# The last tile's expert sums, last C weighting and gating on VectorE, and two experts of the tile before it, in a new instruction order

## The chip, the core and the metric

The kernel runs on one core of a Trainium2 chip. The core's engines take their instructions in order, each from its own queue: TensorE (PE; its weight loads are a row of their own, PEld), VectorE (DVE), ScalarE (ACT), GpSimd (POOL), and SyncE (SP), whose queue issues the DMAs. They meet through semaphores only. The metric is the device time of one execution in microseconds; a kernel's time is the median of its runs.

## What is computed

One layer over x of 32 sequences x 256 tokens x 128 channels, float32: a Mamba block and a mixture of experts, each behind a LayerNorm and with a residual.

```python
# x: (32, 256, 128); 256 inner channels, 16 states, 8 experts of 256 hidden units
xr = layernorm(x) @ W_in;  xi, res = split(xr)
u = silu(causal_conv4(xi) + conv_b)
dbc = u @ W_x                       # delta (rank 8), B (16), C (16)
delta = softplus(dbc[:, :8] @ W_dt + b_dt)
h_t = exp(delta * A) * h_(t-1) + delta * B * u     # for each channel and state
y = sum_n(h * C) + u * D
x = x + (y * silu(res)) @ W_out

s = layernorm(x) @ gate_w.T;  cw = softmax over the top 2 of 8 scores, 0 elsewhere
x = x + sum_e cw[:, e] * (silu(layernorm(x) @ w1[e].T) @ w2[e].T)
```

## The kernel before, in words

**Tiles.** The sequences are cut into 17 tiles: tile 0 and tile 16 hold one sequence (256 tokens), tiles 1 to 15 two (512). A tile's work is cut into pieces with short names, `i:name` for tile i. The text `ORDER` (L47 to L283) is one list of all pieces, written out; L1144 to L1147 run through it, and each piece appends its instructions to its engines' queues. So the order of the list is each engine's order of work, and the relation between engines is set by what waits for what. The order runs three to four tiles side by side: the scans of tile i, the experts of tile i-1, the first half of tiles i+1 and i+2.

**First half.** `ldx` loads x (L373; two buffers, shared with `ldr`, which loads it again for the residual), `st1*`, `sa1`, `rs1`, `ap1` are the LayerNorm (L538 to L563), `tr1`, `hi1`, `nl1`, `lo1` transpose it and split it into a high and a low part, since the large products run as three products of split float32 (`PARTS`). `cv` is the convolution folded into W_in (L635; `km`, `kh`, `kl` prepare its weights, `kw` those of the experts' first layer, `kwr` and `kdt` two others), `u` its SiLU, `gp`, `gs` the gate silu(res), `wx`, `sb`, `rh`, `nr`, `rl`, `zz`, `sp` lead to delta, and `bcd` writes B and C to DRAM, from where `rb` and `rc` load rows of them spread over all partitions (L778; four buffers each).

**Scans.** A tile has 16 scans (tile 0 and 16: 8), each over 1024 elements of 128 partitions. For scan k: `dk` (ScalarE, L760) makes exp(delta*A) into one of nine buffers; `in` (VectorE, L812) multiplies delta*u, held in PSUM, by B; `sc` (VectorE, L819) scans; `cm` (GpSimd, L830) multiplies by C; `ys` (TensorE, L834) adds up in PSUM, transposing. h has three buffers, so a scan waits for the ysum three scans earlier. After each half of the scans `yc` (ScalarE) copies y, `yz` (GpSimd, L911) multiplies it by the gate, `yt` (TensorE) and `ye` (ScalarE) transpose it, `px` and `op` (TensorE, L934 and L941) add the residual and the product with W_out in PSUM, and `x2` (ScalarE, L954) copies the sum.

**Experts.** `st2*`, `sa2`, `rs2`, `ap2`, `tr2`, `hi2`, `nl2`, `lo2` are the second LayerNorm; `gt` (TensorE) the scores; `sc`, `r0` to `r4`, `rx`, `rw0` to `rw4` rank and weigh them on VectorE, GpSimd and, for the exp, ScalarE: rw1 and rw2 (VectorE) wait for rw4 (GpSimd), rw3 (GpSimd) for rw2. For expert e: `wi` (TensorE, L1079, two halves), `si` (ScalarE, L1092), `wo` (TensorE, L1100) into a PSUM tile pe, `as` (ScalarE, L1112) scales pe by the weight into so, one instruction for 128 tokens, and `aa` (GpSimd, L1118) adds so to x2. `sto` stores x2 (L1141). All these PSUM tiles share four buffers of the pool `ps_w`; a new tile takes one that the pieces before it in the list have released.

**Function tables.** ScalarE's exp, SiLU and softplus are in different tables. `need` (L527 to L531) loads one (L530) where the order changes from one to another.

Of the kernel before, what the change touches and what calls it, by code (L numbers as in the profile page):

```python
# [8 lines left out]
F32 = mybir.dt.float32  # L9
# [5 lines left out]
P = 128  # L15
# [32 lines left out]
0:pm 0:ldx 0:lw0 0:lc0 0:lc1 0:ldk 0:lw1 1:ldx 0:ldg 0:st10 0:st11 0:l11 0:sa1 0:ldd 0:rs1 0:ldp 0:km0 0:ap1  # L48
3:ldx 0:tr1 0:l10 0:km1 0:hi1 0:nl1 0:kh1 0:lo1 0:kl1 0:kh0 0:cv1 0:kl0 1:st10 1:st12 1:st13 0:ka 1:st11 1:sa1
1:rs1 0:cv0 0:u1 1:ap1 0:kdt 2:ldx 1:tr1 0:u0 0:kwr 0:wx 0:gp0 0:sb 3:st10 0:rh 0:bcd 1:hi1 0:nr 0:ldo 0:rl  # L50
1:nl1 0:gs0 0:zz 1:lo1 0:pb0 0:kw0 0:sp0 1:cv0 0:pc0 0:rb1 0:rc0 0:rc1 2:st10 0:rb2 0:dq0 0:rb3 2:st13 0:in0
0:rc2 0:rc7 0:ld2 0:dk0 0:kw1 1:cv1 0:dk1 0:sc0 0:dk5 2:st12 0:cm0 0:in1 0:dk2 2:st11 2:sa1 0:sc1 0:dk4 0:kdg
0:rc3 2:rs1 0:ys0 0:dk3 0:in2 0:cm1 0:dk6 0:sc2 0:in3 0:cm2 1:u1 1:u0 3:st11 0:sc3 2:ap1 1:wx 0:ys1 0:dq1 1:rh
0:in6 1:sb 1:bcd 0:ys2 0:sc6 1:nr 1:gp0 1:gs0 1:rl 0:in4 1:zz 0:cm3 1:gp1 1:rb1 3:st13 0:sc4 1:rb5 1:sp0 0:ldr
1:sp1 0:pt 0:ys3 1:du0 0:in5 0:yc0 0:cm4 1:rb4 0:sc5 0:dk7 0:yz0 0:ys4 0:in7 0:kgt 1:dk3 0:cm6 0:yt0 1:dk0
# [232 lines left out]
def mamba_moe_kernel(  # L288
# [938 lines left out]
```

## Time and profile before

| | us |
|---|---|
| median of 3 runs | 1052.45 (1048.1 to 1054.97) |
| the profiled execution | 1053.02 |
| its span, first to last instruction | 1051.3 |
| mean granted TensorE clock | 0.982 of full speed |
| busy: TensorE, weight loads | 964.2, 843.7 |
| busy: VectorE, ScalarE, GpSimd | 956.8, 946.6, 914.0 |
| first scan starts, last scan ends | 28.16, 1012.26 |

A row of a timeline has the start in us, the duration, the engine, the line, the operation, the tile written and those read, their shapes, how many instructions the row holds and, in brackets, how long the engine stood idle before it and what released it. A row with a window has for each engine the busy microseconds and the instructions in it. Durations of pipelined instructions overlap: sixteen output-layer matmuls of 0.28 us take 1.79 us together.

### The profile page before, as it was taken

Reading aid. Unit: us, or ns where it says so; the run is one execution under the profiler, and the core shown is the slowest. Engines: PE = TensorE matmul, PEld = TensorE weight load, DVE = VectorE, ACT = ScalarE, POOL = GpSimd, SP = SyncE. Lnnn points to the kernel's source line nnn. Section 1 sums busy time; section 2 is a strip of 40 time slices with the busy share of each in tenths; the row PEclk is TensorE's granted clock in tenths of the full one; section 3 lists DMA queues with packets and bytes.
Section 4 is the critical chain, followed back from the end, with each engine's and each line's share of the span. In section 5 each row is a group of like instructions: output and inputs, shape, how many; then the busy total and the mean of one; then the engine's idle time right before and its main releaser. Section 6 shows DMA issues by size and latency. Waiting matters only on the chain.

```text
span 1051.3 us, 18971 instructions
## 1 busy us (share of the span) xinstructions
PE 964.2 (92%) x6757; PEld 843.7 (80%) x6757; DVE 956.8 (91%) x903; ACT 946.6 (90%) x1914; POOL 914.0 (87%) x688
## 2 busy tenths in 40 slices
PE   6578789999999999999999999999899999999998
PEld 4467667979888887978888887978778888887898
DVE  3999999999999999999999999999999999999950
ACT  6867989999899998999999898989989998899977
POOL 2577788979989999989999999998989999899975
PEclk9879999999999999999999999999999999999999
DMA  5565848658486775758577684848667584776500
GB/s 180 192 225 173 282 149 281 238 183 275 159 249 220 243 268 192 265 165 283 194 263 247 197 284 140 285 176 282 231 215 252 191 286 159 256 233 201 172 11 17
DMA packets 86095, 223.75 MB, mean 213 GB/s; under 512 B 8049, under 2 KB 35313, under 8 KB 85873
## 3 DMA queue, kind: packets, MB, share of 16 engines
q1 hardware_dynamic: 86000, 222.55, 63.7%
q8 instruction: 53, 0.87, 0.3%
q14 instruction: 42, 0.34, 0.1%
HBM read 217.28 MB, written 5.24 MB: 212 GB/s over the span
## 4 chain that ended last, share of the span: by engine, by line
PE 34%; ACT 29%; DVE 18%; POOL 10%; issue 7%; DMA 1%; SPq 0%; DVEq 0%; POOLq 0%; ACTq 0%
DVE h L819 11%; ACT da L760 11%; PE pf L1079 10%; PE y L834 7%; POOL h L830 6%; PE pe L1100 6%; DVE db L812 6%; ACT L530 5%; ACT so L1112 4%; ACT hs L1092 3%; PE pc L635 3%; POOL x L1118 2%; PE po L941 1%; PE pg L703 1%; PE pd L658 1%
## 5 line engine op out<-in xcount | busy, mean ns | idle before, releaser
L830 POOL TENSOR_TENSOR h<-h,rc 128x1024 f32<-128x1024 f32 x256 | 607.1, 2381 | 62.1 <-DVE h L819 52.2
L819 DVE TENSOR_TENSOR_SCAN h<-da,db 128x1024 f32<-128x1024 f32 x256 | 584.5, 2283 | 25.5 <-PE y L834 7.8
L760 ACT ACTIVATE da<-de,a_sb 128x510 f32<-128x510 f32 (+1 forms) x544 | 341.1, 714 | 0.9 <-DVE h L819 0.4
L812 DVE TENSOR_TENSOR db<-du,rb 128x1024 f32<-128x1024 f32 x256 | 314.9, 1230 | 10.5 <-ACT du L799 2.3
L834 PE MATMUL y<-ident,h 128*128 128x128 f32 x2048 | 268.6, 277 | 16.4 <-POOL h L830 16.0
L834 PEld LDWEIGHTS y<-ident,h 128*128 128x128 f32 x2048 | 237.0, 143 | 37.9 <-POOL h L830 25.7
L1100 PE MATMUL pe<-w_sb,hs 128*128 128x128 f32 x2048 | 249.3, 277 | 9.4 <-ACT so L1112 3.0
L1100 PEld LDWEIGHTS pe<-w_sb,hs 128*128 128x128 f32 x2048 | 237.8, 192 | 16.7 <-ACT so L1112 4.9
L1079 PE MATMUL pf<-xt,w_r 128*128 128x512 f32 (+1 forms) x816 | 215.8, 398 | 14.1 <-DVE rank L1028 6.4
L1079 PEld LDWEIGHTS pf<-xt,w_r 128*128 128x128 f32 x816 | 138.3, 189 | 53.8 <-ACT hs L1092 15.5
L1092 ACT ACTIVATE hs<-pf 128x512 f32<-128x512 f32 (+1 forms) x272 | 143.8, 577 | 40.6 <-PE pf L1079 37.4
L1118 POOL TENSOR_TENSOR x<-x,so 128x512 f32<-128x512 f32 (+1 forms) x136 | 166.0, 1221 | 13.3 <-ACT so L1112 12.3
L1112 ACT ACTIVATE so<-pe,cw 128x128 f32<-128x128 f32 x512 | 147.4, 390 | 4.2 <-PE pe L1100 2.0
L530 ACT ACT_TABLE_LOAD x101 | 129.6, 1283 | 1.8
L635 PE MATMUL pc<-xt_r,wc_r 128*128 128x512 f32 (+1 forms) x408 | 101.0, 399 | 2.7 <-ACT xt_r L624 0.9
L635 PEld LDWEIGHTS pc<-xt_r,wc_r 128*128 128x128 f32 x408 | 74.6, 198 | 18.6 <-issue 2.0
L911 POOL TENSOR_TENSOR g<-yt,g 128x512 f32<-128x512 f32 (+1 forms) x34 | 41.4, 1218 | 7.5 <-ACT yt L904 7.5
L793 POOL TENSOR_TENSOR dus<-de,u 128x512 f32<-128x512 f32 (+1 forms) x32 | 40.3, 1260 | 6.6 <-ACT de L739 6.6
L851 PE MATMUL y<-dg_sb,u 128*128 128x128 f32 x256 | 35.7, 282 | 8.3 <-ACT yt L904 4.2
L851 PEld LDWEIGHTS y<-dg_sb,u 128*128 128x128 f32 x256 | 32.7, 194 | 12.9 <-ACT yt L904 7.5
L941 PEld LDWEIGHTS po<-wo_sb,yt 128*128 128x128 f32 x256 | 31.2, 195 | 4.2 <-issue 2.9
L941 PE MATMUL po<-wo_sb,yt 128*128 128x128 f32 x256 | 32.7, 280 | 0.8 <-ACT yt L922 0.8
(95 smaller groups left out, 705.6 us busy)
## 6 DMA issues: line engine op xcount, KB each, us to landing
rc<-bc SPq DMA_DIRECT2D x205, 512.0 KB, 5.1
rb<-bc SPq DMA_DIRECT2D x187, 512.0 KB, 4.7
xa<-in_x SPq DMA_DIRECT2D x15, 256.0 KB, 4.5
xc<-in_x SPq DMA_DIRECT2D x15, 256.0 KB, 5.5
out<-x SPq DMA_DIRECT2D x15, 256.0 KB, 5.0
w1h<-in_w_t SPq DMA_DIRECT2D x2, 512.0 KB, 5.0
bc<-s SPq DMA_DIRECT2D x32, 32.0 KB, 2.2
w_sb<-in_w_t SPq DMA_DIRECT2D x1, 1024.0 KB, 10.8
```

The lines of the kernel that those rows point to most:

```text
L530: nc.scalar.preload_act_table_set(SETS[which])
L635: nc.tensor.matmul(pcv, wc_r[a][:, j, c * P : (c + 1) * P], xt1_r[b][:, : nb[i], o + j : o + j + L], start=(k == 0), stop=(k == 3 * KC - 1),)
L760: nc.scalar.activation(da[:, m, :, 1:], de[:, :, 1:], AF.Exp, scale=a_sb[:, c, n : n + 1])
L812: nc.vector.tensor_mul(db, d["du"].unsqueeze(1).to_broadcast([P, gs[i], tok[i]]), rows["b", i, k])
L819: nc.vector.tensor_tensor_scan(flat(h), da_of(i, k), flat(d["db"]), 0.0, ALU.mult, ALU.add,)
L830: nc.gpsimd.tensor_tensor(h, h, rows["c", i, k], ALU.mult)
L834: nc.tensor.matmul(y[:, q, :], src[:, q * P : (q + 1) * P], ident, is_transpose=True, start=False, stop=last, skip_group_check=True,)
L1079: nc.tensor.matmul(pf, w1_r[a][:, e, f * P : (f + 1) * P], d["xt"][b], start=(k == 0), stop=(k == 2),)
L1092: nc.scalar.activation(d["hs", e][:, f, :], d["pf", e, f], AF.Silu)
L1100: nc.tensor.matmul(pe[:, q, :], hs[:, f, q * P : (q + 1) * P], w2_sb[:, e, f, :], start=(f == 0), stop=(f == FC - 1),)
L1112: nc.scalar.activation(so[:, q, :], d["pe", e][:, q, :], AF.Copy, scale=d["cw"][:, q, e : e + 1])
L1118: nc.gpsimd.tensor_tensor(x2, x2, st[i]["so", e], ALU.add)
```

## The change

A second form of some pieces is added, and the list is another one throughout. What the last tiles do differently:

- The last scan of tile 16 is weighted by C on VectorE (`cn7`, a new piece) and not on GpSimd (`cm7`).
- The second half's gating in tile 16 is one product on VectorE (`yv1`, new), which reads y from PSUM, in place of ScalarE's copy (`yc1`) and GpSimd's product (`yz1`).
- The eight experts of tile 16, and experts 6 and 7 of tile 15, are weighted and added to x2 by VectorE (`ad`, one scalar_tensor_tensor for each 128 tokens, reading pe from PSUM), in place of `as` on ScalarE and `aa` on GpSimd: 16 + 8 instructions.
- `ad` pieces are now there for all experts. Pieces `st3*`, `xd`, `lv2` and `yv0` and the branch in `op` for a tile without `px` are added too; the list doesn't use them.

All other pieces are in the list as before, at other places. The list is cut here to lines that the text speaks of.

```diff
--- before
+++ after
 ORDER = """
-0:pm 0:ldx 0:lw0 0:lc0 0:lc1 0:ldk 0:lw1 1:ldx 0:ldg 0:st10 0:st11 0:l11 0:sa1 0:ldd 0:rs1 0:ldp 0:km0 0:ap1
-3:ldx 0:tr1 0:l10 0:km1 0:hi1 0:nl1 0:kh1 0:lo1 0:kl1 0:kh0 0:cv1 0:kl0 1:st10 1:st12 1:st13 0:ka 1:st11 1:sa1
-1:rs1 0:cv0 0:u1 1:ap1 0:kdt 2:ldx 1:tr1 0:u0 0:kwr 0:wx 0:gp0 0:sb 3:st10 0:rh 0:bcd 1:hi1 0:nr 0:ldo 0:rl
...
-3:in11 2:rw4 3:cm10 3:ys9 2:rw1 4:sp0 3:rb14 3:sc11 4:sp1 2:wi50 2:wi70 4:du0 3:rc15 3:ys10 2:si70 3:in12
...
-12:as7 13:ys13 13:in15 15:hi1 13:cm14 14:dk0 15:nl1 12:wo2 16:st11 14:rb1 13:sc15 14:rc1 14:dp0 13:ldr 15:lo1
...
-12:wo3 14:rc7 13:st23 14:sc4 12:as0 14:dk12 14:ys2 12:aa4 14:rc5 13:st21 14:dk13 14:ys3 14:in5 14:ldr 14:cm4
...
-15:si50 15:wi51 16:cm4 16:yc0 15:wi31 15:si60 16:sc5 15:wi20 15:si31 15:si51 15:wi70 15:r4 15:si20 16:yz0
-16:ys4 14:aa2 16:in7 15:wi00 15:rx 15:rw4 16:sc7 15:wi11 16:cm5 15:wo5 15:si70 15:si00 15:rw1 15:rw2 16:yt0
-15:rw3 16:px 16:cm7 15:as5 16:ys5 15:si11 16:ys6 16:ye0 15:wi01 14:aa4 16:ys7 15:wo1 14:sto 16:yc1 15:si01
-16:yz1 15:aa5 16:yt1 15:wi21 16:ye1 16:op 15:wo0 16:st20 16:x2 16:st21 15:si21 16:sa2 15:as1 16:rs2 15:wi71
...
-16:si60 16:si40 16:wi50 16:rx 15:as6 15:wo7 16:rw4 15:aa4 16:rw1 16:rw2 16:rw3 15:aa6 16:wi41 16:wo0 16:si50
-15:as7 16:wo2 16:as0 16:wi70 16:si41 16:wi51 16:aa0 16:si70 16:wi71 16:si51 15:aa7 16:wo4 16:si71 16:as2
-16:wi11 16:wo7 15:sto 16:as4 16:si11 16:aa4 16:wi61 16:wo1 16:as7 16:aa2 16:wo5 16:as1 16:aa7 16:si61 16:wo3
-16:aa1 16:as5 16:wo6 16:aa5 16:as3 16:aa3 16:as6 16:aa6 16:sto
...
+0:pt 0:pm 0:ldx 0:lw0 0:lc0 0:lc1 1:ldx 0:ldk 0:ldd 0:ld2 0:lw1 0:st10 0:st11 0:sa1 0:rs1 0:ap1 3:ldx 0:ldo
+0:ldp 0:l11 0:l10 0:km1 0:tr1 0:km0 0:kh1 0:hi1 0:kh0 0:nl1 0:lo1 0:ka 1:st10 1:st13 0:kl1 0:cv1 1:st12 0:kl0
+1:st11 1:sa1 0:kw1 0:kwr 0:kdt 0:cv0 0:u1 1:rs1 1:ap1 1:tr1 0:u0 0:wx 0:kw0 0:gp0 0:sb 0:rh 0:bcd 0:ldg 2:ldx
...
+2:rw0 2:rw4 4:sp0 2:wi40 3:sc11 4:sp1 2:wi50 3:ys10 2:si70 2:si50 2:si21 3:in12 2:rw1 3:cm11 1:aa7 2:wi31
...
+13:ys10 13:dk14 12:rx 12:r2 12:wi31 13:sc11 13:rc13 13:rb14 16:ldx 13:rc14 13:ldr 12:si60 12:si20 12:si31
...
+14:ldr 15:sp0 13:wo2 14:yt0 14:ys13 13:wo7 15:sp1 13:wo1 13:rw2 14:sc14 15:du0 13:rw3 12:aa3 15:dk2 15:dk0
...
+16:cm6 14:aa2 14:sto 16:rc7 15:rw0 16:cm4 16:ys4 15:wi70 15:wi01 16:sc7 16:cn7 15:r4 16:cm5 16:ys5 16:ys6
+15:wi00 16:ys7 15:si70 15:rx 15:rw4 15:rw1 16:yz0 16:yt0 15:rw2 15:rw3 16:yv1 15:si00 15:si01 16:ye0 15:as5
+15:wo1 16:yt1 15:wi21 15:wi61 15:as1 16:px 16:ye1 16:op 15:wo0 16:st20 16:st21 16:sa2 15:aa1 15:aa5 16:rs2
+16:x2 15:si61 15:si21 16:ap2 15:as0 15:aa0 15:wo3 15:wi71 16:tr2 15:wo4 16:hi2 15:si71 15:as3 15:aa3 15:as4
...
+16:si40 15:wo6 15:aa2 16:rw0 16:r4 16:si41 16:wi50 16:si21 16:rx 16:rw4 15:aa4 16:si50 15:wo7 15:ad62 16:rw1
+15:ad60 15:ad63 15:ad61 16:rw2 16:rw3 16:wo0 16:ad00 16:wi11 16:si70 16:wi71 16:si11 16:si71 16:ad01 16:wi51
+16:wi61 16:si61 16:si51 16:wo4 16:wo2 16:wo7 16:ad40 16:ad41 16:wo1 15:ad72 16:ad20 15:ad73 16:ad70 16:ad21
+16:wo5 15:ad71 15:ad70 15:sto 16:ad10 16:wo3 16:ad50 16:ad71 16:wo6 16:ad11 16:ad30 16:ad51 16:ad31 16:ad60
+16:ad61 16:sto
 """
...
@@ -568,7 +569,7 @@
                 scale=d["rs"][:, q : q + 1],
             )
 
-    for n, what, src in (("1", "a", "x"), ("2", "c", "po")):
+    for n, what, src in (("1", "a", "x"), ("2", "c", "po"), ("3", "c", "x2")):
         for q in range(BPT * QL):
             piece(f"st{n}{q}", q, what, src)(ln_stats)
         piece(f"sa{n}", what)(ln_aggr)
@@ -828,6 +829,10 @@
     def weigh(i, k):
         h = st[i]["h", k]
         nc.gpsimd.tensor_tensor(h, h, rows["c", i, k], ALU.mult)
+
+    def weigh_v(i, k):
+        h = st[i]["h", k]
+        nc.vector.tensor_mul(h, h, rows["c", i, k])
 
     def onto_y(y, src, last):
         for q in range(y.shape[1]):
@@ -894,6 +899,7 @@
         piece(f"in{k}", k)(inputs)
         piece(f"sc{k}", k)(scan)
         piece(f"cm{k}", k)(weigh)
+        piece(f"cn{k}", k)(weigh_v)
         piece(f"ys{k}", k)(ysum)
 
     @piece("yc0", 0)
@@ -910,6 +916,15 @@
         yz = d["yz", c] = d["g"][:, :, c * P : (c + 1) * P]
         nc.gpsimd.tensor_tensor(yz, d["yt", c].rearrange("p (q d) -> p q d", d=P), yz, ALU.mult)
 
+    @piece("yv0", 0)
+    @piece("yv1", 1)
+    def _(i, c):
+
+        d = st[i]
+        yz = d["yz", c] = d["g"][:, :, c * P : (c + 1) * P]
+        d["yt", c] = pw.tile([P, tok[i]], F32, tag=f"yt{c}", name=f"yt_{i}_{c}", bufs=1)
+        nc.vector.tensor_tensor(yz, d["y"], yz, ALU.mult)
+
     @piece("yt0", 0)
     @piece("yt1", 1)
     def _(i, c):
@@ -936,13 +951,16 @@
     @piece("op")
     def _(i):
         d = st[i]
+        px = "po" in d
+        if not px:
+            d["po"] = psw(f"po_{i}", tok[i]).rearrange("p (q d) -> p q d", d=P)
         for q in range(nq[i]):
             for c in range(DC):
                 nc.tensor.matmul(
                     d["po"][:, q, :],
                     d["yt", c][:, q * P : (q + 1) * P],
                     wo_sb[:, c, :],
-                    start=False,
+                    start=(c == 0 and not px),
                     stop=(c == DC - 1),
                     skip_group_check=True,
                 )
@@ -952,6 +970,13 @@
         d = st[i]
         x2 = d["x2"] = pw.tile([P, nq[i], P], F32, tag="x2", name=f"x2_{i}", bufs=2)
         nc.scalar.copy(x2, d["po"])
+
+    @piece("xd")
+    def _(i):
+
+        d = st[i]
+        x2 = d["x2"] = pw.tile([P, nq[i], P], F32, tag="x2", name=f"x2_{i}", bufs=2)
+        nc.vector.tensor_tensor(x2, d["po"], d["x"], ALU.add)
 
     @piece("rs2")
     def _(i):
@@ -977,6 +1002,12 @@
     @piece("nl2")
     def _(i):
         less(st[i]["pt"], neg_r, st[i]["xt"][0])
+
+    @piece("lv2")
+    def _(i):
+
+        d = st[i]
+        nc.vector.tensor_tensor(d["xt"][1], d["pt"], d["xt"][0].bitcast(F32), ALU.subtract)
 
     @piece("lo2")
     def _(i):
@@ -1132,9 +1163,8 @@
         if e in ON_ACT:
             piece(f"as{e}", e)(moe_scale)
             piece(f"aa{e}", e)(moe_sum)
-        else:
-            for q in range(BPT * QL):
-                piece(f"ad{e}{q}", e, q)(moe_add)
+        for q in range(BPT * QL):
+            piece(f"ad{e}{q}", e, q)(moe_add)
 
     @piece("sto")
     def _(i):
```

## The prediction

> **What bounds the kernel now.** I began with the busy time of each engine over the whole span, where no engine stands out:
>
> ```profile
> PE 964.2 (92%) x6757; PEld 843.7 (80%) x6757; DVE 956.8 (91%) x903; ACT 946.6 (90%) x1914; POOL 914.0 (87%) x688
> ```
>
> So I cut the span into stages (busy microseconds of each engine; then granted clock, DMA share, GB/s):
>
> ```profile
> 240.00:360.00 120.00, 116.47 (x835) 102.27 (x834) 115.04 (x112) 112.05 (x228) 112.28 (x81) 1.00 0.70 228
> 1000.00:1020.00 20.00, 20.00 (x134) 17.92 (x134) 11.94 (x13) 14.01 (x32) 16.45 (x14) 1.00 0.05 14
> 1020.00:1030.00 10.00, 10.00 (x85) 9.69 (x84) 0.83 (x5) 8.04 (x26) 5.09 (x7) 1.00 0.01 2
> 1030.00:1040.00 10.00, 10.00 (x85) 9.71 (x84) 1.47 (x7) 9.32 (x27) 4.63 (x8) 1.00 0.00 0
> ```
>
> The middle is limited by two engines together: TensorE is 97% busy, VectorE 96%, and 112 VectorE instructions with some 0.04 us of issue between them are most of its other 5 us. Adding up the waits that the timeline marks on VectorE from 60 to 1016 us gives only 20.5 us. From 1000 us on TensorE alone is full and VectorE almost empty. The last rows of the timeline say how it ends (start, duration, line, idle before and its releaser):
>
> ```profile
> 1009.97 2.29 DVE L819 TENSOR_TENSOR_SCAN h<-da,db 128x1024 f32<-128x1024 f32 x1
> 1020.55 0.30 DVE L538 BATCH_NORM_STATS2 st_c<-po 128x6 f32<-128x128 f32 x1 [8.00 <-PE po L941]
> ...
> 1043.24 3.73 PE L1100 MATMUL pe<-w_sb,hs 128*128 128x128 f32 x32
> ...
> 1047.07 0.63 ACT L1112 ACTIVATE so<-pe,cw 128x128 f32<-128x128 f32 x2 [0.26 <-PE pe L1100]
> 1047.84 0.72 POOL L1118 TENSOR_TENSOR x<-x,so 128x256 f32<-128x256 f32 x1 [0.17 <-ACT so L1112]
> ```
>
> The last scan ends at 1012.3, TensorE works without a gap to 1047.0, and ScalarE, GpSimd and the store hang behind it. VectorE's emptiness in the tail is therefore no resource that was missing: **the tail is TensorE's**.
>
> **The tail, part by part.** The profiled execution took 1053.0 us (span 1051.3, 1.7 around it), 0.6 above the median of 1052.45; I sum against 1053.0.
>
> TensorE's list: after tile 16's fourth ysum both orders leave the same pieces. By the rows, a 512-column first layer (wi) is 0.70, a 256-column one 0.35, an output layer (wo) 1.79 or 0.89: 46 us in both. After the gate (16:gt) it is 16 x 0.35 + 8 x 0.89 + 2 x 1.79 = 16.3 in both; the trace has 17.0 (1029.95 to 1046.97). So work taken from ScalarE and GpSimd here buys nothing until TensorE is done. The last C weighting on VectorE (16:cn7): 1.24 by the row L358, a 128x1024 product of the same form, in place of 2.37 on GpSimd after a wait of 0.8; behind it in VectorE's queue stand only rw1 and rw2 of tile 15, which makes that tile's weights about 1 us later. The gating (16:yv1): 0.43 by the 128x256 row L807, in place of copy and product (0.37 + 0.73). Together 3 us off a chain that TensorE's full queue covers (yt1 stands behind 15:wo1, 1.79): I cost it at nothing; without that cover it would be -3.
>
> Expert sums: 24 scalar_tensor_tensor of 128x128 on VectorE. The trace has none of that shape; nearest are L1013 of 128x128 at 0.29 and L498, the same operation on four times the columns, at 0.75. I take 0.30, 7.2 us in all, in 9.5 us of time (at 0.75 they would be 18 us and the bound). What they remove: the last so and x2 additions. From TensorE's end to x2 done is now 1048.56 - 1046.97 = 1.59; then 2 x 0.30 + 0.07 = 0.67. **-0.9** (0 to -0.9).
>
> An added wait: 15:ad62 stands ahead of 16:rw1 and needs GpSimd's 15:aa4 (1.27), which is now behind rw4. With rx one silu later (0.3), rw4 ends at 1036.2, aa4 at 1037.4; then four ads, rw1, rw2 and rw3 put tile 16's weights at 1039.2, against 1037.3 now. All ads queue behind, and with them the PSUM banks that first layers and wo4 take next: 16:wo4 comes up on TensorE at 1040.05, and 16:ad01 frees its bank at 1039.9. One of the four banks stays with 15:wo7 until 15:ad70. **+0.5** (0 to +2).
>
> **The start.** ScalarE's order now has 0:kh1 ahead of 0:hi1, and kh1 waits for the cwb product that ends at 7.56. So lo1, which the first convolution needs, ends at 9.4, not 8.5, and the table load behind it starts at 9.45, not 9.03: +0.4 on the way to the first scan (28.16). The w2 load (1 MB) moves from 24.6 to about 4.2 on SP's queue, ahead of lw1, ldo, ldp and l11. The DMA share is 0.00 from 12 to 16 us, so that is room; wx_sb is needed only at 16.9, and kw1 may wait for l11 ahead of kwr and kdt, which are needed at 18.8 and 21.4. The thr memset goes ahead of pm: 0.45 on an engine that waits 1.6. In return kw0, kw1 and three statistics (2.7 us on VectorE) run before the first scan, and 0:ys1 is ahead of 1:wx, which ends the wait of 0.81 at 44.2. **-1** (-2 to +1).
>
> **Table loads.** Counting where the function set changes along the order: 101 in the old one, as the page has, and 106 in the new; the five are all before tile 3's softplus. A load is 1.28 us and the next instruction starts 0.01 to 0.02 later (1008.66, then 1009.96), so ScalarE gets 5 x 1.29 = 6.5 us. It idles 2.4 to 6.5 us in most stretches of 20 us from 60 to 160, but 0.6 from 100 to 120:
>
> ```profile
> 100.00:120.00 20.00, 13.99 (x108) 12.51 (x107) 18.77 (x14) 19.40 (x32) 15.91 (x11) 0.97 0.82 262
> ```
>
> I take **+1** (0 to +6.5). The Trainium skill ("ScalarE: Activation LUTs", What ACT_TABLE_LOAD costs) speaks against the order more strongly: 1283 ns for the load and about 1380 ns of drain with each switch. By it ScalarE would get 13 us. The load agrees with the trace; the drain isn't there.
>
> **The middle.** Tiles 4 to 14 keep every instruction. Summing row durations, VectorE's work ahead of the fifth, ninth, thirteenth and last scan of each tile differs by at most 0.7 us. GpSimd runs with more than 4 us of other work between two C weightings are 10 before and 8 after; TensorE runs above 4 us between two ysums 48 and 47. So the order is as even as it was. Two stalls lose their cause:
>
> ```profile
> 229.56 0.19 DVE L1062 TENSOR_REDUCE sm<-cw 128x4 f32<-128x32 f32 x1 [1.40 <-POOL cw L1057]
> ...
> 863.20 1.10 PE L934 MATMUL po<-xc,ident 128*128 128x512 f32 x2 [1.15 <-DMA xc<-in_x]
> ```
>
> 2:rw1 comes one scan later, and 13:ldr six scans ahead of 13:px, not two (14:ldr, though, three and not fifteen: 11 us, where 13:ldr's load took 7.9). That is 2.5; new stalls of this kind I can't exclude, since an order moves others near. **-1.5** (-10, half of VectorE's 20.5, to +10 by symmetry).
>
> Sum: 1053.0 - 0.9 + 0.5 - 1 + 1 - 1.5 = 1051.1; **forecast 1051 us**, no change. About 1% (1041.9 to 1063.0) is what a measurement of this kernel can tell from none.
>
> One place where the skill speaks against the change: "GPSIMD Engine Reference" (8. Key points) says that GpSimd shares its SBUF interfaces with VectorE and contends with VectorE instructions that have two SBUF inputs. 16:cn7 has two. The trace has one such overlap (GpSimd's product at 41.90 took 2.46, not 2.36, beside VectorE's at 41.73). By the rule GpSimd loses up to 1.2 us once, behind TensorE.
>
> **Rivals.**
> *Late inputs (slower).* The first statistics of tiles 5, 6, 7, 9 and 11 move from behind scan inputs 10 to 13 to behind inputs 5 to 7, while their loads stand about where they were, behind row loads that wait for buffers on SP. A load lands in 4.6 us, at most 7.1, by the xa rows. If the lead is under about 5 us, VectorE stands still, and all behind it: 2.5 us for each of five, 12.5, so 1053 + 12.5 = 1065.5. Against: no statistic waits for a load after 20 us now, and most leads I count are two scans (7.4 us) or more; tile 5's is near the point (row load behind GpSimd, some 1 us short).
> *Cleared stalls (faster).* Three quarters of the 20.5 us on VectorE go, 15, with the tail's -0.9: 1037. For: they are small waits whose producers all moved. Against: the counts above are equal.
> *It doesn't do what it says.* VectorE's sums save nothing, the later weights eat the 0.9, the other terms cancel: 1053.
>
> **How the numbers follow.** Forecast 0.68 (its own range 1045 to 1058; 0.03 of it below 1042, 0.01 above 1063), late inputs 0.13, cleared stalls 0.12, nothing 0.07. Faster by over 1%: 0.12 + 0.03 = 0.15; slower 0.13 + 0.01 = 0.14; within 0.71. The range goes from 1039 to 1064: the upper half of the cleared-stall case and half of the late-input case lie inside, about 0.15 outside.
>
> **What would show it.** Right: TensorE full from 1000 us; one so less at the end, two short VectorE rows of 0.3 and the store 0.9 earlier after the last matmul; 106 table loads; no wait of rw1 near 230 and of po near 863; VectorE's marked waits still near 20 us. Wrong: statistics waiting for xa, wi or wo waiting for VectorE's ads after 1037, scans waiting for da between 60 and 180 us, or a first scan later than 29 us.

## The result, and the profile after

The changed kernel takes 1055.6 us (median of 19 runs, 1053.21 to 1058.8), the kernel before 1053.07 (19 runs, 1047.79 to 1055.21). The ratio is 1.003, 95% interval 1.0016 to 1.0044: 0.3% slower, well within the 1% that was called no change, but on the other side of zero than the forecast of 1051. The profiled execution took 1056.61 us with a span of 1054.8, so 3.5 us more than the span before (1051.3).

The busy times of the engines on the page of the changed kernel:

```profile
PE 965.6 (92%) x6757; PEld 845.6 (80%) x6757; DVE 966.0 (92%) x929; ACT 945.0 (90%) x1894; POOL 902.5 (86%) x676
```

VectorE has 9 us more, ScalarE 1.6 and GpSimd 11.5 less, as the change moves work. Nothing in this line explains 3.5 us. The stages do (busy microseconds of each engine; then granted clock, DMA share, GB/s):

```profile
240.00:360.00 120.00, 116.78 (x832) 101.87 (x830) 114.98 (x110) 111.36 (x224) 111.69 (x80) 1.00 0.69 227
480.00:540.00 60.00, 55.71 (x384) 48.36 (x383) 52.98 (x52) 50.97 (x107) 51.96 (x38) 0.97 0.64 204
1000.00:1020.00 20.00, 18.78 (x119) 15.83 (x118) 16.42 (x16) 14.02 (x30) 15.97 (x13) 1.00 0.13 40
1020.00:1030.00 10.00, 10.00 (x78) 9.26 (x77) 1.14 (x5) 6.89 (x23) 4.25 (x7) 1.00 0.01 2
1030.00:1040.00 10.00, 10.00 (x88) 9.88 (x87) 1.14 (x5) 8.72 (x28) 3.88 (x6) 1.00 0.00 0
```

The middle from 240 to 360 us is as full as before. From 480 to 540 us every engine loses 3 to 6 us at once; the same window of the kernel before reads

```profile
480.00:540.00 60.00, 58.41 (x429) 52.37 (x427) 58.81 (x55) 55.35 (x113) 57.43 (x41) 1.00 0.68 234
```

When all engines fall together, one of them waited and the others followed. To see where in the order that is, I cut both spans at the starts of scans. The columns are differences of such starts in the profiled executions; the last column is a kernel from the experiments, in which the waits for x2 are gone.

| stretch | before | changed | changed without waits for x2 |
|---|---|---|---|
| to the first scan | 28.16 | 26.37 | 26.43 |
| to the first scan of tile 4 | 220.52 | 218.18 | 217.64 |
| to that of tile 8 | 245.16 | 244.83 | 244.81 |
| to that of tile 9 | 60.20 | 65.84 | 61.01 |
| to that of tile 16 | 427.89 | 428.79 | 425.88 |
| to the end of the last scan | 30.33 | 33.64 | 32.84 |
| to the end of the span | 39.04 | 37.10 | 37.08 |
| span | 1051.3 | 1054.8 | 1045.7 |

The changed kernel is 4.5 us ahead when tile 8 begins and 1.2 us behind when it ends. VectorE's timeline of the changed kernel shows the place (start, duration, line, idle before and its releaser):

```profile
500.69 0.50 DVE L539 BATCH_NORM_STATS2 st_c<-po 128x6 f32<-128x128 f32 x2 [0.35 <-PE po L959]
501.10 2.27 DVE L820 TENSOR_TENSOR_SCAN h<-da,db 128x1024 f32<-128x1024 f32 x1
506.84 0.50 DVE L539 BATCH_NORM_STATS2 st_c<-po 128x6 f32<-128x128 f32 x2 [3.46 <-ACT x L972]
...
520.96 0.19 DVE L1037 COPY sc<-psc 128x32 f32<-128x32 f32 x1 [1.41 <-PE psc L1026]
```

The last two statistics of tile 7 (7:st22, 7:st23) wait 3.46 us, and what ends the wait is ScalarE's x2, the copy of the same PSUM tile po. Both only read po. In the list 7:x2 now stands ahead of 7:st22. Before, it stood behind all four statistics, and the last three of them had no wait, though ScalarE came to its copy only 3.6 us after they had begun:

```profile
507.13 0.67 DVE L538 BATCH_NORM_STATS2 st_c<-po 128x6 f32<-128x128 f32 x3
```

```profile
510.73 0.59 ACT L954 COPY x<-po 128x512 f32<-128x512 f32 x1
```

ScalarE's timeline of the changed kernel shows why x2 was late:

```profile
501.59 1.27 ACT L1143 ACTIVATE so<-pe,cw 128x128 f32<-128x128 f32 x4
502.59 1.49 ACT L761 ACTIVATE da<-de,a_sb 128x510 f32<-128x510 f32 x2
503.82 1.29 ACT L1143 ACTIVATE so<-pe,cw 128x128 f32<-128x128 f32 x4
504.82 1.51 ACT L761 ACTIVATE da<-de,a_sb 128x510 f32<-128x510 f32 x2
506.04 0.76 ACT L972 COPY x<-po 128x512 f32<-128x512 f32 x1
```

ScalarE never idles here; x2 is behind exps and expert scales in its queue, and VectorE, with nothing of its own missing, waits for the end of that queue. TensorE then runs dry behind VectorE, and its rows show a second loss:

```profile
514.15 1.45 PE L839 MATMUL y<-ident,h 128*128 128x128 f32 x8 [2.95 <-POOL h L831]
515.38 1.06 PE L580 MATMUL pt_c<-ident,xn_c 128*128 128x128 f32 x4
516.38 1.94 PE L659 MATMUL pd<-u,wx_sb 128*64 128x256 f32 x8
```

Four transposes of 128x128 mostly take 0.60 to 0.66 us at full clock, here 1.06: after the pause the granted clock is 0.5 from 514.7 to 518.1 us. The window shows both, the pause and the clock:

```profile
510.00:520.00 10.00, 7.05 (x45) 5.31 (x44) 9.32 (x7) 4.60 (x10) 9.92 (x7) 0.83 0.14 54
```

Behind pause and halved clock the scores come 1.41 us late for VectorE (the row at 520.96); how much of it is the clock's alone isn't separated. 3.46 and 1.41 are 4.9 of the 5.6 us that this tile costs.

The end is TensorE's, as before, but not as short. From tile 16's first scan to the end of the span it is 70.7 us, before 69.4: VectorE waits once more for an x2, tile 15's, and the last scan waits for a ysum:

```profile
994.80 0.89 DVE L539 BATCH_NORM_STATS2 st_c<-po 128x6 f32<-128x128 f32 x4 [1.12 <-ACT x L972]
...
1015.36 2.29 DVE L820 TENSOR_TENSOR_SCAN h<-da,db 128x1024 f32<-128x1024 f32 x1 [2.28 <-PE y L839]
```

TensorE is busy from 1008.4 us to its end, but for 0.13 us, and short VectorE rows and the store stand behind it:

```profile
1044.76 6.56 PE L1131 MATMUL pe<-w_sb,hs 128*128 128x128 f32 x56
```

```profile
1049.50 2.47 DVE L1154 SCALAR_TENSOR_TENSOR x<-pe,cw,x 128x128 f32<-128x128 f32 x8 [0.48 <-PE pe L1131]
```

TensorE's end (1051.32, before 1046.97) to the span's end is 3.48 us, before 4.33.

### The profile page after: what moved, and what is told of

Same layout as the page of the kernel before. It is cut to its first block, busy times and chain, and to the rows that moved or that the text cites. A ratio compares the mean times of both kernels' runs of the same rounds, so it can differ in the third digit from the quotient of the medians.

```text
span 1054.8 us, 18962 instructions
## 1 busy us (share of the span) xinstructions
PE 965.6 (92%) x6757; PEld 845.6 (80%) x6757; DVE 966.0 (92%) x929; ACT 945.0 (90%) x1894; POOL 902.5 (86%) x676
## 4 chain that ended last, share of the span: by engine, by line
ACT 38%; PE 35%; DVE 13%; POOL 8%; issue 6%; DMA 0%; SPq 0%; DVEq 0%; POOLq 0%; ACTq 0%
ACT da L761 15%; PE pf L1110 11%; DVE h L820 8%; PE y L839 7%; ACT so L1143 6%; ACT L531 6%; PE pe L1131 5%; POOL h L831 4%; DVE db L813 4%; ACT hs L1123 3%; PE pc L636 3%; PE psc L1026 1%; POOL x L1149 1%; PE po L959 1%; ACT de L740 1%
## 5 line engine op out<-in xcount | busy, mean ns | idle before, releaser
L839 PE MATMUL y<-ident,h 128*128 128x128 f32 x2048 | 269.7, 278 | 22.3 <-POOL h L831 21.9
L839 PEld LDWEIGHTS y<-ident,h 128*128 128x128 f32 x2048 | 237.6, 144 | 41.4 <-POOL h L831 30.2
L1149 POOL TENSOR_TENSOR x<-x,so 128x512 f32<-128x512 f32 (+1 forms) x126 | 157.6, 1251 | 16.6 <-ACT so L1143 14.9
L1143 ACT ACTIVATE so<-pe,cw 128x128 f32<-128x128 f32 x488 | 140.9, 401 | 3.2 <-POOL x L1149 1.7
```

Source lines behind the costliest of these rows:

```text
L839: nc.tensor.matmul(y[:, q, :], src[:, q * P : (q + 1) * P], ident, is_transpose=True, start=False, stop=last, skip_group_check=True,)
L1143: nc.scalar.activation(so[:, q, :], d["pe", e][:, q, :], AF.Copy, scale=d["cw"][:, q, e : e + 1])
L1149: nc.gpsimd.tensor_tensor(x2, x2, st[i]["so", e], ALU.add)
```

## The experiments

The theory: a statistic of po that the list has behind x2 waits for x2, however late ScalarE comes to it, because two engines' readings of one PSUM tile are put in the order of the list; VectorE's standstill in the full middle is lost, and TensorE's clock adds to it. The rivals: the pause is taken up by slack before the end, since the tail is TensorE's; or the loss is elsewhere (the five table loads, the tail's new pieces, the start) and tile 8 only shows it.

### Moving x2 of tile 7

In the changed list, x2 goes behind the statistics:

```diff
-7:st21 8:sc3 8:dk12 7:x2 7:st22 7:st23 8:in4
+7:st21 8:sc3 8:dk12 7:st22 7:st23 7:x2 8:in4
```

> The changed kernel with one piece moved: 7:x2 (ScalarE's copy of po) stands behind 7:st23 in the list and not ahead of 7:st22. Theory A: VectorE's wait of 3.46 us at 503.4 (ended by x2) is what the change lost; the wait goes, VectorE's scans of tile 8 stay about 4.5 us ahead of the kernel before as they were until then, and the span falls from 1054.8 to 1050 to 1051.5, about 0.995 to 0.998 of the time of the kernel before. Theory B: VectorE is not what sets the end (TensorE has work left from 1012 us on), the next wait takes the stall's place, and the span stays within 1 us of 1054.8.

Measured: median 1052.12, ratio to the kernel before 0.9986 (0.9972 to 1.0), span 1048.3. VectorE's timeline has no wait there any more, and TensorE is full at full clock in the window that follows:

```profile
501.73 0.47 DVE L543 BATCH_NORM_STATS2 st_c<-po 128x6 f32<-128x128 f32 x2
503.24 0.37 DVE L549 BATCH_NORM_AGGREGATE mv_c<-st_c 128x2 f32<-128x6 f32 x4
```

```profile
510.00:520.00 10.00, 10.00 (x65) 7.83 (x64) 9.49 (x9) 7.57 (x18) 9.76 (x8) 1.00 0.31 112
```

The scans of tile 8 take 59.45 us, not 64.25: 4.8 us, by one piece put two places later. They are kept to the end: tile 16 begins 6.5 us earlier, and nearly all of the other 1.7 arises before tile 3, where the stretches of halved clock lie differently in the two executions. Theory A; the tail doesn't swallow the pause. That the span is below the stated 1050 is owed to those 1.7 us, not to the edit.

The opposite, in the list of the kernel before:

```diff
-8:ys1 7:st22 8:dk12 7:st21 7:st23 8:in4 9:cv1 8:cm3 8:rc7 6:as4 7:sa2 8:sc4 8:dk11 7:rs2 8:rc12 8:ys2 7:x2 8:in5
+8:ys1 8:dk12 6:as4 7:x2 7:st22 7:st21 7:st23 8:in4 9:cv1 8:cm3 8:rc7 7:sa2 8:sc4 8:dk11 7:rs2 8:rc12 8:ys2 8:in5
```

> The kernel before with x2 of tile 7 listed ahead of its last three statistics (8:dk12 and 6:as4 are listed ahead of x2, so that ScalarE's own order changes only by x2 passing 8:dk11). Theory A: the statistic at 507.13 now waits for x2, which ScalarE reaches at about 509.6, so VectorE stands still some 3 us; the span grows by 3 to 4.5 us over 1051.3. Theory B: the pause is taken up by slack before the end, and the span grows by less than 1 us.

```profile
510.14 0.69 DVE L542 BATCH_NORM_STATS2 st_c<-po 128x6 f32<-128x128 f32 x3 [3.38 <-ACT x L975]
```

The wait appears, 3.38 us long, and the scans of tile 8 take 61.89 us, not 58.41: 3.5 us more. TensorE's clock stays at 1.00 there and the scores are not waited for, so the loss is the wait alone; in the changed kernel it was the wait and the late scores behind it. The span is 1053.6, 2.3 us longer and under the stated 3, since this execution was 0.4 us ahead when tile 8 began and gains 0.7 in tiles 9 to 15. The median is 1055.69 and the ratio 1.0012 (0.9993 to 1.0031), which alone would not settle it; the tile's own time does.

### x2 moved up in ScalarE's queue

The changed list, x2 ahead of the exps and scales that delayed it, the statistics still behind it:

```diff
-6:aa7 8:dk4 8:dk7 8:dk10 6:as3 8:dk11 6:as4 11:ldx 8:rb7 8:rb6 7:st21 8:sc3 8:dk12 7:x2 7:st22
+6:aa7 7:x2 8:dk4 8:dk7 8:dk10 6:as3 8:dk11 6:as4 11:ldx 8:rb7 8:rb6 7:st21 8:sc3 8:dk12 7:st22
```

> The changed kernel with 7:x2 put up in ScalarE's queue, ahead of 8:dk4, 8:dk7, 8:dk10, 6:as3, 8:dk11, 6:as4 and 8:dk12; the statistics st21 to st23 stay behind x2 in the list. Theory A (the wait of 3.46 us is the time that x2 stood behind these seven pieces, some 8 us of ScalarE's work): x2 is done before VectorE comes to the statistics, the wait is under 0.7 us and tile 8's scans take 59.3 to 60.2 us, not 64.25. Rival (that two engines read po costs the time, or op is late): the wait stays over 2 us.

The rows are TensorE's, ScalarE's and VectorE's:

```profile
498.41 1.95 PE L963 MATMUL po<-wo_sb,yt 128*128 128x128 f32 x16
```

```profile
500.73 0.59 ACT L976 COPY x<-po 128x512 f32<-128x512 f32 x1 [2.86 <-DVE st_c L543]
```

```profile
501.35 0.30 DVE L543 BATCH_NORM_STATS2 st_c<-po 128x6 f32<-128x128 f32 x1 [0.65 <-ACT x L976]
```

VectorE's wait for x2 falls to 0.65 us, as theory A said. But the tile takes 61.41 us, between the two forecasts. Now ScalarE stands 2.86 us ahead of its copy. 2.5 us of that is owed to the product op, which TensorE ends at 500.36 only; for the last 0.4 the copy waits for VectorE's statistic 7:st20 (500.39 to 500.69), which the list has ahead of it. So the order holds the other way too, though here it costs little: the reader of po that comes second in the list waits for the first. VectorE waits for no exp in this tile; its further waits are 0.63 us for GpSimd's product (513.38) and 0.93 for the scores (517.86), and how ScalarE's pause leads to them was not followed. Median 1051.67, ratio 0.9996 (0.9977 to 1.0015).

The Trainium skill has this rule, and I had not weighed it: "PSUM — Partial Sum Buffer", section "PSUM bank collisions raise a hardware error", says that a schedule must order any two accesses of different engines to one PSUM bank and the same partitions, a ScalarE read against a VectorE read included. The rows agree: in the kernel before x2 ends a wait of VectorE's only in tiles 2, 9, 13 and 16, which are among those whose list has a statistic behind x2, and in the changed kernel in tiles 0, 7, 8, 9, 13 and 15, which are all of those.

### All six

The changed list with x2 of tiles 0, 7, 8, 9, 13 and 15 behind the last statistic; tile 8's, for one:

```diff
-9:dk10 8:x2 9:dk8 9:dk11 7:as7 9:dk9 8:st20 9:sc3 9:dk12 10:u0 8:st21 8:st23 9:in4 8:st22 9:sc4
+9:dk10 9:dk8 9:dk11 7:as7 9:dk9 8:st20 9:sc3 9:dk12 10:u0 8:st21 8:st23 9:in4 8:st22 8:x2 9:sc4
```

> The changed kernel with x2 of tiles 0, 7, 8, 9, 13 and 15 moved behind the last of their statistics. The waits that x2 ends in the changed kernel add up to 7.5 us (3.46, 1.12, 0.96, 0.70, 0.62, 0.61). Theory A: all go, and the span falls to 1047 to 1050. Rival: the small ones are only the time in which VectorE would have waited for ScalarE or TensorE anyway, or a later x2 delays the apply step behind it, and the span is that of the run with one x2 moved, 1050 to 1051.5.

Measured: median 1046.82, ratio 0.9939 (0.9918 to 0.996), span 1045.7: **faster than both kernels**, and lower than theory A's 1047. Beyond tile 7 the gain is 0.8 us in tile 9's scans, 2.0 in tile 14's and 0.8 in tile 16's. Tile 14's 2.0 is more than its wait (0.70): in the changed kernel a half-clock stretch of 3.4 us follows at 890.2, and there is none in this profile.

To learn whether this is the waits or the rest of the new order, the same was done to the list of the kernel before, in tiles 2, 3, 5, 9, 13 and 16, and the changed list was run again beside it:

```diff
-1:as5 2:x2 2:st22 3:in4
+1:as5 2:st22 2:x2 3:in4
...
-4:sc3 3:x2 2:as5 4:dk10 4:rc5 3:st22 4:cm3 3:st23 3:st21 2:wo7
+4:sc3 2:as5 4:dk10 4:rc5 3:st22 4:cm3 3:st23 3:st21 3:x2 2:wo7
```

> The kernel before with x2 of tiles 2, 3, 5, 9, 13 and 16 moved behind the last of their statistics, as was done in the changed list. The waits that x2 ends there add up to 2.06 us before the tail (0.60, 0.65, 0.81). Theory A (the old order pays the same price, only less of it): span 1049.2 to 1050.5, and the changed list without these waits (1045.7) stays 3 to 5 us ahead, which is what the rest of the new order is worth. Rival (the old order had set x2 there because scalar work behind it is urgent): span 1051 to 1053.

> The changed list with x2 behind the statistics everywhere once more, beside the run above on the same chip. If its 0.9939 rests on the waits, the ratio is again 0.992 to 0.997 and the tile 8 and tile 14 take 59.4 and 58.3 us; if it came from a lucky clock in its few runs, the ratio is 0.997 to 1.000.

The old list so mended: median 1052.46, ratio 0.9992 (0.9976 to 1.0009), span 1051.0. The changed list: median 1047.18, ratio 0.9944 (0.9924 to 0.9964), which is the first figure again. So the old list had little to gain: 13 of its statistics stand behind x2, in the changed list 17, but x2 ended only 2.06 us of waits there. The span of 1051.0 lies in the rival's range, but this execution begins its scans 2.0 us later than the one before (30.13, behind four stretches of halved clock), and from tile 4 to tile 16 it takes 732.0 us, before 733.3; a gain of 1 us is not excluded. The new order without its six misplaced copies is worth 0.5%. The repeat's profiled execution has a span of 1049.8: tile 15 takes 61.96 us, not 59.09, behind two half-clock stretches at 945.6 us that the first profile doesn't have.

### The tail

The old list up to 16:gt, and the changed list's pieces from there on (expert sums on VectorE):

```diff
 16:lo2 15:as4
-16:gt 15:as2 16:wi20 16:sc 16:wi30 16:r3 16:r0 16:si20
...
-16:as6 16:aa6 16:sto
+16:gt 15:as2 16:wi20 16:sc 16:wi30 16:r3 16:r0 16:r1
...
+16:rx 16:rw4 15:aa4 16:si50 15:wo7 15:ad62 16:rw1 15:ad60 15:ad63 15:ad61 16:rw2 16:rw3 16:wo0 16:ad00
...
+16:ad60 16:ad61 16:sto
```

> The kernel before with only the pieces behind 16:gt taken from the changed list: the eight expert sums of tile 16 and those of experts 6 and 7 of tile 15 on VectorE, in the changed kernel's order; everything ahead of 16:gt, 16:cm7, 16:yc1 and 16:yz1 too, as before. Theory A: TensorE stays full and ends at 1047.0 as before, the two last steps behind it are shorter, span 1051.3 - 0.75 = 1050.5. Rival: the wait of 15:ad62 for GpSimd's 15:aa4 makes TensorE wait for a bank, and the span is 1051.3 to 1053.

Median 1051.44, ratio 0.9982 (0.9961 to 1.0003). The profiled span, 1052.2, holds two half-clock stretches in tile 15 that are 80 us ahead of the edit; from the end of 16:gt to the end of the span it is 20.7 us (1031.48 to 1052.2), before 21.35 (1029.95 to 1051.3). That is -0.6, near theory A's 0.75. In the changed kernel it is 20.75.

The last C weighting and the gating alone, in the old list:

```diff
-16:px 16:cm7 15:as5
+16:px 16:cn7 15:as5
...
-14:sto 16:yc1 15:si01 16:yz1 15:aa5
+14:sto 16:yv1 15:si01 15:aa5
```

> The kernel before with only 16:cn7 at the place of 16:cm7 and 16:yv1 at the place of 16:yc1, 16:yz1 left out. Theory A (the forecast: TensorE's queue is full from 1000 us, so it is worth nothing): from the last scan's end to the end of the span 39.0 us as before (1051.3 - 1012.3), span 1050.8 to 1051.6 apart from shifts that are there before 900 us. Theory B: TensorE had been waiting in ways that its rows hide, and up to 3 us are gained.

From the end of the last scan (1013.80) to the end of the span (1053.0) it is 39.2 us, before 39.04; TensorE has no gap behind 1000.2 us. Median 1052.03, ratio 0.9992 (0.9974 to 1.0009). In the old order these pieces are worth nothing, as the forecast costed them (its first scan is 2.0 us later, at 30.16, which the span of 1053.0 holds).

The reverse, old pieces in the new order. A first try put 16:cm7 at the place of 16:cn7, and that is ahead of 16:cm5 in GpSimd's queue:

```diff
-16:sc7 16:cn7 15:r4 16:cm5 16:ys5 16:ys6 15:wi00 16:ys7
+16:sc7 16:cm7 15:r4 16:cm5 16:ys5 16:ys6 15:wi00 16:ys7
...
-15:rw3 16:yv1 15:si00
+15:rw3 16:yc1 16:yz1 15:si00
```

> The same kernel (span 1045.7) with the old pieces at the end of tile 16's scans: 16:cm7 on GpSimd at the place of 16:cn7, and 16:yc1, 16:yz1 at the place of 16:yv1. Theory A (TensorE's full queue covers the chain, as the forecast costs it): span within 0.7 us of 1045.7, no new gap on TensorE between 1000 us and its end. Theory B (the cover is gone in the new order): TensorE waits for ysum 7 or for yt1, up to 3 us, span 1047 to 1048.7.

Span 1057.4, ratio 1.0075 (1.0052 to 1.0097): far outside both forecasts, because 16:cm5 waited for the last scan in that queue and TensorE stood 5.94 us for it (and 2.15 behind it). It measures my placing, not the pieces. With 16:cm7 behind 16:cm5:

```diff
-16:sc7 16:cn7 15:r4 16:cm5 16:ys5
+16:sc7 15:r4 16:cm5 16:cm7 16:ys5
```

> The kernel with x2 behind the statistics everywhere (span 1045.7) with the old pieces at the end of tile 16's scans, this time 16:cm7 behind 16:cm5 in GpSimd's queue (it stood ahead of it in the run before, and 16:cm5 waited for the last scan); 16:yc1 and 16:yz1 at the place of 16:yv1. Theory A (TensorE's full queue covers the chain in this order too): span within 0.7 us of 1045.7. Theory B (this order leaves TensorE nothing else between ysum 6 and ysum 7): TensorE waits for the slower product and the gating, 1.1 to 3 us, span 1046.8 to 1048.7.

TensorE's timeline has two gaps that the changed list doesn't have:

```profile
1010.68 1.09 PE L843 MATMUL y<-ident,h 128*128 128x128 f32 x8 [1.02 <-POOL h L835]
1014.14 2.98 PE L1135 MATMUL pe<-w_sb,hs 128*128 128x128 f32 x16 [2.13 <-ACT hs L1127]
```

The first is ysum 7, which waits for GpSimd's slower product. The second is less the gating's length than its place in ScalarE's queue: 15:wo1 starts at 1014.14, when the silu 15:si00 is done, and that silu stands behind the copy yc1, which waits for ysum 7, and behind a table load:

```profile
1011.81 0.37 ACT L914 COPY yt<-y 128x256 f32<-128x256 f32 x1 [3.13 <-PE y L843]
1012.20 1.28 ACT L535 ACT_TABLE_LOAD   x1
1013.49 1.08 ACT L1127 ACTIVATE hs<-pf 128x512 f32<-128x512 f32 x2
```

Span 1050.3 against 1045.7, ratio 1.0 (0.9984 to 1.0016): 4.6 us, more than theory B's 3, since the clock is halved from 1015.0 on (sixteen output matmuls in 2.98 us, elsewhere 1.95). "Worth nothing" holds for one order: at these places in the new one the old pieces cost 4.6 us. Whether another place for yc1 would spare some of it was not tried.

### Table loads

All further runs are edits of the changed list without the waits for x2 (span 1045.7). Ten more loads, each of the table that is in already, behind ten pieces from 1:gs0 to 2:dk11 (0:tl is the new piece):

```diff
-1:sp1 1:gs0
+1:sp1 1:gs0 0:tl
...
+    @piece("tl")
+    def _(i):
+        nc.scalar.preload_act_table_set(SETS[table[0]])
```

> The changed kernel with x2 behind the statistics everywhere (span 1045.7) and ten more function table loads on ScalarE, each right behind a piece that has just loaded the same table, spread between tile 1's and tile 3's softplus (about 30 to 170 us). Ten loads of 1.283 us are 12.9 us of ScalarE's time, twice the five that the change adds. Theory A (a load is hidden there, as the forecast's +1 for five says): span 1046 to 1049, and ScalarE's idle time between 30 and 180 us falls by 10 us or more. Theory B (ScalarE sets the pace there): span 1055 to 1059.

Median 1062.42, ratio 1.0098 (1.0076 to 1.012), span 1061.1; tile 3 begins 12.3 us later, and tile 15 loses 2.8 more at 957 us, where the clock is halved in this execution. Theory B: ten loads cost about their own time, 12.8 us, though the 12.3 also hold a halved clock at 86.7 us that the list's own profile doesn't have. VectorE's timeline has the waits in two places above all:

```profile
92.85 2.29 DVE L824 TENSOR_TENSOR_SCAN h<-da,db 128x1024 f32<-128x1024 f32 x1 [5.53 <-PE y L843]
...
151.47 0.30 DVE L543 BATCH_NORM_STATS2 st_c<-po 128x6 f32<-128x128 f32 x1 [4.81 <-PE po L963]
```

Neither names ScalarE: TensorE waits for ScalarE (1.54 us up to 84.99, 5.02 up to 145.95) and once for VectorE's ranking (1.76 up to 87.37), and VectorE for TensorE. The five loads of the change itself had not cost that: the changed kernel reaches tile 4's first scan 2.3 us sooner from its first scan on than the kernel before, and the one wait that follows a load is 0.88 us (the scan at 88.52). So I took four of them out, by moving two lone pieces:

```diff
-1:dk12 0:rx 2:cv0
+1:dk12 1:dk7 0:rx 2:cv0
...
-0:si70 1:dk7 1:in7
+0:si70 1:in7
...
-2:ys0 3:u1 2:dk9
+2:ys0 2:dk9 3:u1
```

> The kernel with x2 behind the statistics everywhere (span 1045.7; 106 table loads) with 1:dk7 moved up behind 1:dk12 and 3:u1 behind 2:dk9: two lone pieces between pieces of another table, so four loads fewer, 102. Ten loads more cost 13 us there. Theory A (the loads that the change added were nearly covered; only the one ahead of the scan at 88.1 made VectorE wait, 0.89 us): span 0.5 to 1.5 us less, 1044.2 to 1045.2. Theory B (every load in this stretch costs its own time, as the ten did): 5 us less, 1040 to 1041.

Median 1050.91, ratio 0.9984 (0.9968 to 0.9999), span 1049.1: both were wrong, it is 3.4 us slower with four loads fewer. VectorE's row:

```profile
91.51 2.29 DVE L824 TENSOR_TENSOR_SCAN h<-da,db 128x1024 f32<-128x1024 f32 x1 [3.97 <-PE y L843]
```

and TensorE's, a little earlier:

```profile
87.60 1.65 PE L708 MATMUL pg<-wr_r,xt_r 128*128 128x256 f32 x6 [2.69 <-DVE rank L1063]
```

TensorE waits 2.69 us for a PSUM tile that VectorE's ranking of tile 0 holds, and its clock is halved at 87.5. With 1:dk7 earlier, the ScalarE pieces behind it come up to 1.2 us later (u at 82.48, not 81.27). Which of them held the ranking up is not settled. What is shown: in this stretch a load is not priced by itself, and a lone exp between two others' tables can be cheaper than the order that saves its loads.

### The start

ScalarE's first pieces in an order nearer to the old one, so that the convolution can begin 1 us earlier:

```diff
-0:tr1 0:km0 0:kh1 0:hi1 0:kh0 0:nl1 0:lo1 0:ka
+0:tr1 0:km0 0:hi1 0:nl1 0:kh1 0:lo1 0:kh0 0:ka
```

> The same kernel (span 1045.7) with ScalarE's and TensorE's start put nearer to the old order: 0:hi1, then 0:kh1, 0:lo1, and 0:kh0 behind them, 0:nl1 behind 0:hi1. The convolution then starts some 1 us earlier than at 10.2. Theory A (the forecast's step: lo1 is on the way to the first scan): first scan 0.4 to 1 us earlier than at 26.4, at 25.4 to 26.0. Theory B (TensorE's clock decides): TensorE then waits for tile 1's xn before tr1, as it did in the kernel before from 13.67 to 15.35, its clock is halved from about 16 us for one stretch of 3.4 us, and the first scan is at 26.9 to 27.9.

```profile
9.20 4.53 PE L640 MATMUL pc<-xt_r,wc_r 128*128 128x256 f32 x24 [1.49 <-ACT xt_r L629]
14.43 1.48 PE L584 MATMUL pt_a<-ident,xn_a 128*128 128x128 f32 x4 [0.69 <-ACT xn_a L568]
```

The convolution starts at 9.2. That is hardly earlier than in the profile of the list it edits (9.43); the 10.2 was the changed kernel's. TensorE waits 0.69 us for tile 1's xn, and the first scan is at 26.61, not 26.43. Neither theory's number is met. What the eleven profiles with the new start do show: the convolution starts anywhere from 9.2 to 10.9, and the first scan is at 26.4 to 26.9 all the same (10.20 goes with 26.37, 9.43 with 26.43). So lo1 isn't on the way, and in this run a gap of 0.69 us doesn't halve the clock. Median 1048.53, ratio 0.997 (0.995 to 0.9989), and the span of 1049.9 has its further 4 us from tile 4 on, with halved stretches at 886.2 and 947.7 us.

### First statistics of po one scan later

In tiles 1, 2, 6, 7 and 14; tile 6's:

```diff
-6:op 7:in3 6:st20 7:sc3 6:st22 6:st21 6:st23
+6:op 7:in3 7:sc3 6:st20 6:st22 6:st21 6:st23
```

> The same kernel (span 1045.7) with the first statistics of po in tiles 1, 2, 6, 7 and 14 (those that waited 0.71, 0.42, 0.41, 0.35 and 0.65 us for TensorE's op) put behind the next scan, x2 of tile 1 behind its statistics. Theory A (a wait of VectorE's in the middle is lost time one to one): 2 to 2.5 us less, span 1043.2 to 1043.7. Theory B (the statistics come later, and so do apply and scores; or TensorE sets the pace): span within 1 us of 1045.7.

Median 1048.96, ratio 0.9982 (0.9965 to 0.9998), span 1046.1: nothing gained, theory B; the ratio is even 0.4% above that of the list it edits. In tile 7 the scans are 0.31 us shorter, where the wait was 0.44; in tile 3 they are 0.58 longer, a scan now waiting 0.97 us for its ysum. A wait taken away is kept only where nothing of the same length is due next; the 3.46 of tile 7 was, the small ones were not.

## Why the prediction was wrong, step by step

- **What bounds the kernel**: right. The middle is VectorE's and TensorE's together, the tail is TensorE's, which ran full to 1051.3. (That VectorE is almost empty holds from 1012 us on; the forecast's own window from 1000 to 1020 has it 60% busy.)
- **Expert sums, -0.9**: right. From TensorE's end to the span's end 4.33 became 3.48, so -0.85, and the instruction takes 0.30 to 0.35 us, 0.30 taken.
- **Later weights, +0.5**: right in mechanism, +0.25 in size. From the end of 16:gt to that of 16:rw3 it is 9.35 us, before 7.35, the 2 us that were worked out; TensorE's time from 16:gt to its end grew from 17.02 to 17.27.
- **C weighting and gating, nothing**: right for the old order (39.2 against 39.04 us behind the last scan). It was asked of the old order only; in the new one the old pieces, at the places tried, cost 4.6 us.
- **The start, -1**: right in sign and within its bounds (-1.8), wrong in mechanism. The +0.4 for lo1 isn't there; what went, as far as the rows show, is a half-clock stretch from 16.4 to 19.8 us, which none of the terms held.
- **Table loads, +1**: not settled. One wait, of 0.88 us, follows one of the loads, but no run took the five out alone, and the run with four fewer was slower. The upper bound of 6.5 had a reason: ten more cost some 12 us, so the cover ended there. At tile 4 the changed kernel was 4.1 us ahead (244.55 against 248.68), where the start, the loads and the first of the two stalls make 1.4 at most. That was luck, and it hid part of the miss.
- **The middle, -1.5**: this step failed. From the start of tile 4 to that of tile 16 it is 733.25 us before and 739.46 after, +6.2; without the waits for x2 it is 731.70, so -1.55. That this meets -1.5 is luck: one of the two stalls lies ahead of tile 4, and executions of one list differ by more (731.7 and 735.1 without the waits). The two stalls that were named are gone, as forecast, but "the order is as even as it was" counted the work between scans and the runs of GpSimd and TensorE, and gave new stalls 1 us in the sum and 10 in the range. It didn't look at pairs of readers of one PSUM tile, and there the lists differ: a statistic stands behind x2 in six tiles in both, but in the new list in tile 7 with a full ScalarE queue ahead of x2. The waits that x2 ends rose from 2.06 to 7.47 us, of 20.5 and 28.1 us in all (from 1.5 to 5.7 between these two tiles), and the scores that came late behind pause and halved clock added 1.4.
- **The tail's sum, -0.4**: missed. From tile 16's first scan to the end it is 1.4 us more (70.7 against 69.4), and 0.6 more without the waits for x2 (69.95). The terms for the expert sums and the later weights were right in kind for what stands behind 16:gt; but TensorE has 499 matmuls to do from that scan on, before 485, and the forecast had counted its work only from the fourth ysum on.
- **The rivals**: no statistic waits for a load of x after 60 us, so late inputs fell out. The slower outcome came by a wait that was in the trace of before, three rows of 0.60 to 0.81 us released by x2, the longest

```profile
872.06 0.30 DVE L538 BATCH_NORM_STATS2 st_c<-po 128x6 f32<-128x128 f32 x1 [0.81 <-ACT x L954]
```

  They were small, and I added them into the 20.5 without asking what would make them long.

## What to carry to other kernels

When an order is changed, list the pairs of instructions on different engines that touch the same PSUM tile, reads too: as with po here, the second one waits for the first, wherever the first stands in its queue. A small wait in the old trace is a dependence whose length the order sets, so ask what stands ahead of the releaser in the new one. And price a pause of TensorE with its clock: in the changed kernel the 3.4 us behind a pause of 3 us ran at half speed.

## What the runs showed of the hardware that was not expected

- **The clock is granted in stretches of 3.4 us, and one with TensorE under 40% busy was always followed by half clock.** In the changed kernel TensorE was 16% busy from 511.3 to 514.7 us, and the next stretch was granted 0.5. The Trainium skill ("TensorE: Matmul & The Clock Gate", What's actually happening) gives windows of about 3.4 us and an idle window as the condition. The windows agree; the condition is wider here: the stretch at 886.8 us of the kernel before is halved (0.50 in the window from 886.8 to 890.2) though TensorE was 86% busy in the one before it, with score matmuls of 8 columns among the work. Counted over all sixteen profiles from 25 us on: of 87 stretches with TensorE under 40% busy all were followed by half clock, of the 4725 others 81. What decides for those 81 is open.
- **The start of the old list loses its clock again, that of the new list doesn't.** Both begin at half speed: the 128x256 matmuls of the convolution take 0.42 us each, up to 13.0 us in the kernel before and to its end in the changed one, and 0.28 later. (The clock column reads 1.00 there, since the profile has no record ahead of the first full stretch, which begins at 13.0 and 16.4 us.) Windows of the kernel before (TensorE first, granted clock third from the end), behind a gap of TensorE's from 13.67 to 15.35:

```profile
16.00:17.00 1.00, 0.89 (x4) 0.41 (x4) 0.00 (x0) 0.82 (x3) 0.00 (x0) 0.71 0.00 0
17.00:18.00 1.00, 1.00 (x3) 0.60 (x4) 0.00 (x0) 0.00 (x0) 0.00 (x0) 0.50 0.22 67
```

  In the changed kernel TensorE's rows have no gap there (its convolution ends at 15.66, tr1 starts at 15.46), and the clock, once full, stays:

```profile
16.00:17.00 1.00, 1.00 (x6) 0.56 (x5) 0.98 (x2) 0.37 (x2) 0.00 (x0) 1.00 0.00 0
17.00:18.00 1.00, 0.95 (x6) 0.52 (x5) 0.95 (x3) 0.42 (x2) 0.00 (x0) 1.00 0.00 0
```

  The rows behind the gap are longer for it, the projection's above all (first the kernel before, then the changed one):

```profile
16.92 1.97 PE L658 MATMUL pd<-u,wx_sb 128*64 128x256 f32 x4
```

```profile
16.46 1.08 PE L659 MATMUL pd<-u,wx_sb 128*64 128x256 f32 x4
```

  In all five profiles with the old list's start the clock, full from 11.9 to 13.1 us on, is halved again after one stretch, from 15.3 to 16.5 us on, for one to four stretches, and the first scan is at 27.4 to 30.2, latest (30.1) in the two with four. In the eleven with the new start it isn't halved again before 21.9, and the first scan is at 26.4 to 26.9. That the gap is the cause was argued from these rows; no run took it out by itself.
- **A part of what differs between executions of one kernel is such stretches.** The same list took 59.09 and 61.96 us for tile 15 in two executions, the second with two halved stretches at 945.6. A stage is therefore better compared by its own scans than by the span.
- **A GpSimd instruction beside a VectorE product with two SBUF operands took up to 1 us longer.** In the run with the new gating in the old list, the two rows below overlap (the first is VectorE's, the second GpSimd's):

```profile
1014.00 1.46 DVE L838 TENSOR_TENSOR h<-h,rc 128x1024 f32<-128x1024 f32 x1
```

```profile
1014.32 1.23 POOL L1105 TENSOR_TENSOR cw<-cw,sm 128x32 f32<-128x32 f32 x1
```

  The same instructions take 1.23 (1017.68) and 0.23 (1019.67) in the changed kernel, where they don't overlap each other. There the VectorE product meets another small GpSimd product, which takes 0.79 us (1018.23) against 0.25 in the run with the new gating in the old list (1011.79); VectorE's own 1.23 is not longer. The forecast had weighed the rule of the Trainium skill ("GPSIMD Engine Reference", 8. Key points) by one overlap, which cost GpSimd 0.1 us; a small GpSimd instruction can lose 1 us. TensorE's queue covered it here.
